# A second mixture with three sets of groups as rows by expert, the first of them placed and sent inside the attentions

## The chip, the cores and the metric

The kernel runs on one core of one Trainium2 chip. The metric is the time of one execution on the device in microseconds (us). Nine runs of the kernel before lie between 1503.12 and 1531.77 us, with a median of 1510.65.

## The reference

A decoder of two layers works on 32 batches of 128 tokens with 128 features, in float32. Each layer is three sub-layers with a residual each: a self-attention, a cross-attention with a context, and a mixture of experts. The change is in the mixture of the second layer, and in when its first part is prepared:

```python
x2 = hidden_states.reshape(-1, 128)                  # 4096 tokens, after the layer norm
logits = x2 @ gate_w.T                               # 16 experts
_, sel = top_k(logits + expert_bias, 4)
rw = softmax(logits taken at sel)                    # 4 shares for each token
out = swiglu(x2, shared) + sum over e of g[:, e] * swiglu(x2, expert e)   # g: rw put at sel
```

`swiglu(x, wg, wd, wu)` is `silu(x @ wg.T) * (x @ wu.T) @ wd.T`, with matrices of 128 x 128. Every token needs only 4 of the 16 experts; the reference computes them all and multiplies by the share, which is 0 for the other 12.

## The kernel before

**Units.** 4 batches (512 tokens) are a *group*, 8 groups in all; 2 groups (8 batches, `NBR`) are a *set*, sets 0 to 3. The residual `x[g]` of every group stays in SBUF.

**Dense or by rows.** The last layer has two ways to compute the mixture.
- *Dense*: for each group 16 *chunks*, one per expert. A chunk (`chunk_up`, `chunk_down`) is three products of a 128 x 128 matrix with the group's 512 columns (`pg`, `pu`, `y`), an ACT `Silu`, and two DVE products, the second with the `share` of the expert, which is loaded from DRAM already repeated over the partitions (`fetched`, 1 MB for four experts). A 17th chunk is the shared expert.
- *By rows*: the tokens of a set are copied to places ordered by expert. Routing on DVE (`route_rows`) gives four experts and shares per token; `placed` works out 4 places for each token with a chain of small PE and DVE operations and the expert that owns each tile of 128 rows (`owner`). `way_out` sends the tokens with 32 indirect DMAs (four for each batch, issued by POOL) to `rows_in` in DRAM. That table has 48 tiles of 128 rows, 12 *quads* of four tiles. For each quad `rows_of` loads four tiles (256 KB) and, after reading the owner of each tile into an SP register, that expert's three matrices (192 KB a tile), all on SP's queue; `rows_turned`, `rows_up` and `rows_down` transpose (`prows`), multiply by three matrices (`pg`, `pu`, `pyrows`, 128 columns per tile) and store to `rows_out` (on ACT's queue). `way_back` fetches each token's four results with 32 more indirect DMAs, and `added` multiplies by the shares and adds them to `x` on DVE. The group's shared chunk is still needed (`alone`).

Before the change sets 1 and 2 go by rows (`SETS = (1, 2)`), sets 0 and 3 are dense.

**Order.** `steps` writes the order of the instructions out by hand: a list of stages, each with its first step, its distance and its count; `between` stages are filled in piece by piece between the others. In `last_layer` steps 0 to 14 take two dense chunks each while sets 1, 2 and 3 are normed (`norm`, `scaled`), turned (`turn`), routed (`routing`, `chosen`), placed and sent; from step `Q0 = 15` on each step takes one quad and one dense chunk; then the rest of the dense chunks and the `alone` ones follow. Set 0 is routed (softmax) and its shares written to DRAM inside `second_layers`, the steps of the two attentions of the second layer, so that its dense chunks can start when the attentions end. In those attentions POOL copies the values to their spread form (`v`, line 1070), computes factors of norms (`r`), half of the normed tiles, and a check of the reciprocals (`in_range`, line 1309).

**Lines.** 974 is the helper `mm` of most matmuls, 1115 and below the helpers of the norms; 1290 to 1297 the averages of the attention; 2000 to 2033 the routing by rows, 2045 to 2077 the placing, 2080 the owners, 2088 the scatter, 2101 and 2109 the loads of rows and weights, 2117 to 2140 the quads, 2145 the gather, 2156 the adding, 2167 to 2170 the dense chunk.

Of the kernel before, what the change touches and what calls it, by code (L numbers as in the profile page):

```python
# [10 lines left out]
I32 = mybir.dt.int32  # L11
# [944 lines left out]
def fast_decoder(ctx: ExitStack, tc: tile.TileContext, ins, spans, out: bass.AP):  # L956
# [6 lines left out]
    st = ctx.enter_context(tc.tile_pool(name="st", bufs=4))  # L963
    kinds = {}
# [39 lines left out]
    F = load("fast", nc.sync)  # L1004
    ident = K["ident"]


    def load_wide(eng, *names):
        t = res.tile([128, sum(ins[n].shape[1] for n in names)], F32, name="wide")
        at, out = 0, []  # L1010
        for n in names:
            part = t[:, at : at + ins[n].shape[1]]
            at += ins[n].shape[1]
            out.append((_Pieces(part, spans[n]), lambda part=part, n=n: eng.dma_start(out=part, in_=ins[n])))
        return out

    (W0X, load_w0x), (W0F, load_w0f) = load_wide(nc.sync, "w0x", "w0f")
# [18 lines left out]
    ones_by_4 = res.tile([128, 4, 4 * HD], F32, name="ones_by_4")  # L1036
# [762 lines left out]
    def mixture(tag, W, route, per, last, weights_of):  # L1799
# [10 lines left out]
        def scaled(wk, g):  # L1810
            xn[g] = yield from normed(wk, g, *xn[g])
# [89 lines left out]
    def mixture_layer(tag, stages, more=()):  # L1901
# [36 lines left out]
    SETS = (1, 2)  # L1938
    NT = 4 * NBR + E
    QUADS = NT // 4  # L1940
    tables = ctx.enter_context(tc.tile_pool(name="tables", bufs=1, space=bass.MemoryType.DRAM))
    rows_in, rows_out = (
        {n: tables.tile([NT * S, D], F32, name=f"{name}{n}") for n in SETS} for name in ("rows_in", "rows_out")
# [10 lines left out]
    def last_layer(tag, W, stages, of_expert):  # L1954

        wk = phase(tag, mixture_psum)
        C = load("last", nc.scalar, wk)
        send, made = stages[5], stages[-1]
        hs, shares, NS = made["hs"], {}, made["NS"]
        one = wk.tile([128, 1], F32, name="one", bufs=1)  # L1960
        nc.vector.memset(one, 1.0)
        factors, xn, choices, ones, masks, parts, places, owners, held, ys, sgs, outs = ({} for _ in range(12))
# [5 lines left out]
        def scaled(g):  # L1968
            xn[g] = wk.tile([128, GB, D], F32, name="xr", bufs=2 * len(SETS) + 2)
            yield from normed(wk, g, *factors.pop(g), xn[g], nc.vector)  # L1970
# [14 lines left out]
        def routing(n):  # L1985
            lg = sm([128, NBR, E], "logits")
            for i, g in enumerate(of_set(n)):
                for b in range(GB):
                    mm(lg[:, i * GB + b, :], lhsT=hs[g][:, bass.ts(b, S)], rhs=W["r"], start=True, stop=True)
            choices[n] = route_rows(lg, n) if n in SETS else route_softmax(lg, edge)  # L1990
            next(choices[n])
# [6 lines left out]
        def route_rows(lg, n):  # L1998
            s = wk.tile([128, NBR, E], F32, name="s", bufs=1)
            nc.vector.tensor_copy(s, lg)  # L2000
            yield
            v = wk.tile([128, NBR, E], F32, name="v", bufs=1)
            nc.vector.tensor_tensor(v, s, rep(P["expert_bias"], NBR, 1), ALU.add)
            yield
            best = yield from greatest(v)

            ones[n] = wk.tile([128, 4, NBR, E], F32, name="ones", bufs=1)
            for k in range(4):
                nc.vector.tensor_tensor(ones[n][:, k], v, rep(best[:, :, k], E, 2), ALU.is_equal)
                yield  # L2010

            mask = masks[n] = wk.tile([128, NBR + 1, E], F32, name="mask", bufs=1)
            nc.vector.memset(mask[:, NBR], 0.0)
            nc.vector.tensor_tensor(mask[:, 0:NBR], v, rep(best[:, :, 3], E, 2), ALU.is_ge)
            yield
            raw = parts[n] = wk.tile([128, 4, NBR], F32, name="parts", bufs=len(SETS))
            t = wk.tile([128, 4, NBR, E], F32, name="picked", bufs=1)
            nc.vector.tensor_tensor(t, ones[n], rep(s, 4, 1), ALU.mult)
            yield
            nc.vector.tensor_reduce(raw, t, AX.X, ALU.add)  # L2020
            yield
            by_batch = raw.rearrange("p k b -> p b k")
            top = st.tile([128, NBR], F32, name="rtop")
            nc.vector.tensor_reduce(top, by_batch, AX.X, ALU.max)
            nc.vector.tensor_tensor(raw, raw, rep(top, 4, 1), ALU.subtract)
            yield
            nc.scalar.activation(raw, raw, AF.Exp)
            yield
            den = st.tile([128, NBR], F32, name="den")
            nc.vector.tensor_reduce(den, by_batch, AX.X, ALU.add)  # L2030
            nc.vector.reciprocal(den, den)
            yield
            nc.vector.tensor_tensor(raw, raw, rep(den, 4, 1), ALU.mult)

        def placed(n):

            mask = masks.pop(n)

            pp = sm([128, NBR + 1, E], "places")
            mm(pp, lhsT=C["below"], rhs=mask, start=True, stop=False)  # L2040
            for b in range(NBR):
                rhs = rep(mask[:, b], NBR - b, 1)
                mm(pp[:, b + 1 :], lhsT=one.to_broadcast([128, 128]), rhs=rhs, start=False, stop=(b == NBR - 1))
            pos = wk.tile([128, NBR + 1, E], F32, name="pos", bufs=1)
            nc.vector.tensor_copy(pos, pp)
            yield
            tiles = wk.tile([128, E], F32, name="expert_tiles", bufs=1)
            t = wk.tile([128, E, 8], F32, name="over", bufs=1)
            nc.vector.tensor_tensor(t, rep(pos[:, NBR], 8, 2), rep(C["tiles"], E, 1), ALU.is_gt)
            yield  # L2050
            nc.vector.tensor_reduce(tiles, t, AX.X, ALU.add)
            yield
            ends = wk.tile([128, E], F32, name="expert_ends", bufs=1)
            t = wk.tile([128, E, E], F32, name="upto", bufs=1)
            nc.vector.tensor_tensor(t, rep(K["desc16"], E, 1), rep(K["desc16"], E, 2), ALU.is_ge)
            yield
            nc.vector.tensor_tensor(t, t, rep(tiles, E, 1), ALU.mult)
            yield
            nc.vector.tensor_reduce(ends, t, AX.X, ALU.add)
            yield  # L2060
            nc.vector.tensor_tensor(tiles, ends, tiles, ALU.subtract)
            slot = pos[:, 0:NBR]
            nc.vector.scalar_tensor_tensor(slot, rep(tiles, NBR, 1), float(S), slot, ALU.mult, ALU.add)
            yield
            t = wk.tile([128, 4, NBR, E], F32, name="picked", bufs=1)
            nc.vector.tensor_tensor(t, ones.pop(n), rep(slot, 4, 1), ALU.mult)
            yield
            slots = wk.tile([128, 4, NBR], F32, name="slots", bufs=1)
            nc.vector.tensor_reduce(slots, t, AX.X, ALU.add)
            yield  # L2070
            places[n] = wk.tile([128, 4, NBR], I32, name="place", bufs=len(SETS))
            nc.vector.tensor_copy(places[n], slots)
            yield
            nc.vector.tensor_scalar(ends, ends, C["row"], None, ALU.is_le)  # L2074
            of = wk.tile([128, 1], F32, name="of", bufs=1)
            nc.vector.tensor_reduce(of, ends, AX.X, ALU.add)
            nc.vector.tensor_scalar(of, of, E - 1.0, None, ALU.min)
            yield
            pt = sm([1, S], "powner")
            nc.tensor.transpose(pt, of, ident)  # L2080
            owners[n] = wk.tile([1, S], I32, name="owner", bufs=len(SETS))
            nc.vector.tensor_copy(owners[n], pt)


        def way_out(n, u):
            b, g = u % GB, n * NBR // GB + u // GB
            for k in range(4):
                sent = nc.gpsimd.indirect_dma_start(  # L2088
                    out=rows_in[n],
                    out_offset=bass.IndirectOffsetOnAxis(ap=places[n][:, k, u : u + 1], axis=0),  # L2090
                    in_=xn[g][:, b],
                    in_offset=None,
                )

                tc.declare_no_dep(sent.ins, group=f"rows{n}", reason="rows of different places")
                tc.add_to_no_dep_group(f"rows{n}", sent.ins)
                nc.gpsimd.nop()
# [92 lines left out]
        at = {}  # L2190
        Q0 = 15
        todo = list(dense)
        for s in range(Q0):
            at[s] = [todo.pop(0) for _ in range(2)]
        s = Q0
        while s < Q0 + len(quads) + 1 and todo:
            at[s] = [todo.pop(0)]
            s += 1
        while todo:
            at[s] = [todo.pop(0) for _ in range(min(2, len(todo)))]  # L2200
            s += 1
        s = max(s, Q0 + len(quads) + 1)
# [409 lines left out]
```

## Time and profile before

| | |
|---|---|
| median of nine runs | 1510.65 us |
| the profiled execution | 1512.41 us, span 1510.6 us |
| PE busy | 1311.5 us (87%) |
| DVE, ACT, POOL busy | 874.0, 575.9, 470.5 us |
| moved by DMA | 114.41 MB, 76 GB/s over the span |
| indirect DMAs on POOL | 64 to `rows_in`, 64 from `rows_out` |
| mean granted TensorE clock | 0.938 |

The profile is of one execution. A row of a time line gives the start in us, the length, the engine, the source line, the operation, out<-in, and in brackets how long the engine was idle before and what ended that. "remote" stands where no recorded operation ends the wait. `PEld` is the weight load of PE, which lies beside its matmuls. A float32 matmul is recorded as two.

The first layer ends and the mixtures change at about 800 us; from 800 to 1104 us run the two attentions of the second layer, and from 1104 to the end the last layer.

### The profile page before, as it was taken

Reading aid. Unit: us, or ns where it says so; the run is one execution under the profiler, and the core shown is the slowest. Engines: PE = TensorE matmul, PEld = TensorE weight load, DVE = VectorE, ACT = ScalarE, POOL = GpSimd, SP = SyncE. Lnnn points to the kernel's source line nnn. Section 1 sums busy time; section 2 is a strip of 40 time slices with the busy share of each in tenths; the row PEclk is TensorE's granted clock in tenths of the full one; section 3 lists DMA queues with packets and bytes.
Section 4 is the critical chain, followed back from the end, with each engine's and each line's share of the span. In section 5 each row is a group of like instructions: output and inputs, shape, how many; then the busy total and the mean of one; then the engine's idle time right before and its main releaser. Section 6 shows DMA issues by size and latency. Waiting matters only on the chain. (4 is left out here: it accounts for less than half of the span.)

```text
span 1510.6 us, 27025 instructions
## 1 busy us (share of the span) xinstructions
PE 1311.5 (87%) x10598; PEld 842.8 (56%) x10598; DVE 874.0 (58%) x2256; ACT 575.9 (38%) x846; POOL 470.5 (31%) x665
## 2 busy tenths in 40 slices
PE   3699999999999986999998998898797474997896
PEld 2367777777777764444444665665443242765643
DVE  5656767768686653865754667675466252333453
ACT  2354545454454332333323455554531121332321
POOL 5324343333422311310001444542205425004343
PEclk7799999999999997999999999999898686999998
DMA  9201211111121124354152000000042302897812
GB/s 346 62 1 30 55 33 30 30 30 30 30 48 40 30 56 98 69 113 91 33 103 89 2 2 2 2 1 2 1 159 88 99 16 101 261 271 216 243 52 65
DMA packets 90422, 114.41 MB, mean 76 GB/s; under 512 B 7664, under 2 KB 73840, under 8 KB 87856
## 3 DMA queue, kind: packets, MB, share of 16 engines
q1 hardware_dynamic: 71936, 95.24, 23.1%
q0 software_dynamic: 4096, 8.40, 1.9%
q10 hardware_dynamic: 14256, 8.97, 1.9%
q8 instruction: 86, 1.41, 0.4%
q14 instruction: 48, 0.39, 0.1%
HBM read 93.05 MB, written 19.53 MB: 75 GB/s over the span
## 5 line engine op out<-in xcount | busy, mean ns | idle before, releaser
L974 PE MATMUL y<-sg,wide 128*128 128x512 f32 x288 | 156.3, 630 | 25.3 <-DVE sg L2170 18.2
L974 PE MATMUL pg<-hx,wide 128*128 128x512 f32 x288 | 154.1, 617 | 17.6 <-issue 16.2
L974 PE MATMUL pu<-hx,wide 128*128 128x512 f32 x288 | 152.1, 610 | 3.7 <-DVE sg L2168 3.7
L1275 ACT ACTIVATE e<-scores 128x1024 f32<-128x1024 f32 x128 | 124.0, 1021 | 56.9 <-PE scores L974 56.9
L2168 DVE TENSOR_TENSOR sg<-sg,pu 128x512 f32<-128x512 f32 x72 | 49.3, 685 | 141.5 <-PE pu L974 79.9
L2145 POOL DMA_INDIRECT back<-rows_out,place x64 | 62.6, 977 | 161.8 <-PE pg L974 88.9
L974 PEld LDWEIGHTS y<-sg,wide 128*128 128x128 f32 x288 | 49.8, 197 | 94.3 <-DVE sg L1880 36.3
L1121 POOL TENSOR_SCALAR xn<-x,mv,r 128x128 f32<-128x128 f32 x84 | 70.8, 850 | 91.6 <-PE pxn L1130 82.8
L1290 DVE STREAM_TRANSPOSE by_token<-sums 128x512 f32<-128x512 f32 x64 | 45.6, 713 | 91.7 <-PE sums L974 91.4
L974 PEld LDWEIGHTS pu<-hx,wide 128*128 128x128 f32 x288 | 55.9, 196 | 75.2 <-issue 67.5
L2167 ACT ACTIVATE sg<-pg 128x512 f32<-128x512 f32 x72 | 42.6, 597 | 139.7 <-PE pg L974 83.8
L1526 ACT ACTIVATE e<-xscores 128x1024 f32<-128x1024 f32 x64 | 62.0, 1021 | 79.9 <-PE xscores L974 79.9
L974 PEld LDWEIGHTS pg<-hx,wide 128*128 128x128 f32 x288 | 53.2, 199 | 66.5 <-issue 62.6
L974 PE MATMUL scores<-qb,k 32*128 32x512 f32 x512 | 78.2, 682 | 12.0 <-ACT qb L1461 4.5
L1877 ACT ACTIVATE sg<-pg 128x512 f32<-128x512 f32 x72 | 43.0, 597 | 119.0 <-PE pg L974 110.1
L974 PE MATMUL sums<-e,v 128*32 128x128 f32 x2048 | 74.5, 287 | 12.7 <-POOL v L1070 10.6
L1878 DVE TENSOR_TENSOR sg<-sg,pu 128x512 f32<-128x512 f32 x72 | 49.3, 685 | 60.8 <-PE pu L974 58.1
L2088 POOL DMA_INDIRECT rows_in<-xr,place x64 | 62.3, 973 | 65.0 <-DVE expert_ends L2074 46.1
L974 PEld LDWEIGHTS sums<-e,v 128*32 128x32 f32 x2048 | 55.4, 114 | 41.5 <-issue 16.5
L1092 POOL TENSOR_SCALAR r<-mv 128x4 f32<-128x4 f32 x48 | 11.5, 240 | 208.3 <-DVE mv L1111 207.9
L974 PE MATMUL po<-e,v 128*64 128x128 f32 x1024 | 66.2, 281 | 8.9 <-DVE v L1540 8.9
L1574 ACT COPY av<-po 128x512 f32<-128x512 f32 x64 | 37.5, 586 | 90.8 <-PE po L974 90.7
(280 smaller groups left out, 2769.2 us busy)
## 6 DMA issues: line engine op xcount, KB each, us to landing
row_weights<-in_w1f_dram SPq DMA_DIRECT2D x96, 192.0 KB
factor<-factors SPq DMA_DIRECT2D x64, 256.0 KB
share<-combined SPq DMA_DIRECT2D x32, 512.0 KB
share<-combined SPq DMA_DIRECT2D x16, 1024.0 KB
rows_in<-in_few SPq DMA_DIRECT2D x24, 256.0 KB
rows<-rows_in SPq DMA_DIRECT2D x24, 256.0 KB
rows_out<-yrows ACTq DMA_DIRECT2D x24, 256.0 KB
wide<-in_w1f_dram SPq DMA_DIRECT2D x1, 3272.0 KB
```

Source lines behind the costliest of these rows:

```text
L974: last[0] = nc.tensor.matmul(*args, **kw)
L1121: eng.tensor_scalar(n[:, b, :], x[g][:, b, :], mv[:, b, 0:1], r[:, b : b + 1], ALU.subtract, ALU.mult)
L1275: nc.scalar.activation(e[-1], ps[:, bass.ts(n, 2)].rearrange("p c i s -> p (c i) s"), AF.Exp, scale=scale)
L1290: nc.vector.transpose(tt.rearrange("p i t r -> p (i t r)"), po.rearrange("p i s -> p (i s)"))
L1526: nc.scalar.activation(e[-1], ps[:, n].rearrange("p r c s -> p (r c) s"), AF.Exp, scale=scale)
L1574: nc.scalar.copy(avs[w][n][:, :, bass.ts(b, S)], po)
L1877: nc.scalar.activation(sg, pg, AF.Silu)
L1878: nc.vector.tensor_tensor(sg, sg, pu, ALU.mult)
L2088: sent = nc.gpsimd.indirect_dma_start(out=rows_in[n], out_offset=bass.IndirectOffsetOnAxis(ap=places[n][:, k, u : u + 1], axis=0), in_=xn[ ...
L2145: nc.gpsimd.indirect_dma_start(out=outs[n, u][:, k], out_offset=None, in_=rows_out[n], in_offset=bass.IndirectOffsetOnAxis(ap=places[n][:, ...
L2167: nc.scalar.activation(sg, pg, AF.Silu)
L2168: nc.vector.tensor_tensor(sg, sg, pu, ALU.mult)
```

## The change

`SETS` becomes `(0, 2, 3)`; set 1 alone is dense. The tables, the routing and the placing move from `last_layer` into a class `Tables`, whose tiles lie in pools that live across both stages; the placing's large temporaries take buffers of the first attention (`rot`, `rotsin`), and set 0's normed tokens lie in the unused end of the `wide` weight tile. Set 0 is routed by rows, placed and sent inside `second_layers` (`placed` at step 37, `owned` and `way_out` from 39 on); its shares are no longer sent to DRAM. In `last_layer` the quads of set 0 start at step 1; sets 2, 1 and 3 are normed, turned, routed, and sets 2 and 3 placed and sent, beside them; the dense chunks of set 1 start at step 8, one per step to 23, one in three steps to 36, then two per step; six shared chunks end it. `filled`, which initializes `rows_in` in the first layers, has three tables instead of two (12 more DMAs of 256 KB). Some constants move to a pool that is closed after the first layers.

```diff
-    SETS = (1, 2)
+    SETS = (0, 2, 3)
...
+        def kept(self, g):
+            self.xn[g] = self.spare[:, g]
+            return self.xn[g]
...
+            ones, t = self.two_wide()
+            self.ones[n] = ones, t
...
         dense = [(g, c) for g in range(NG) if g * GB // NBR not in SETS for c in range(E + 1)]
         alone = [(g, E) for g in range(NG) if g * GB // NBR in SETS]
         quads = [(n, q) for n in SETS for q in range(QUADS)]
-        at = {}
-        Q0 = 15
-        todo = list(dense)
-        for s in range(Q0):
-            at[s] = [todo.pop(0) for _ in range(2)]
-        s = Q0
-        while s < Q0 + len(quads) + 1 and todo:
-            at[s] = [todo.pop(0)]
-            s += 1
-        while todo:
+        NQ = len(quads)
+
+        at, todo = {}, list(dense)
+        for s in range(8, NQ + 1):
+            if s < 2 * QUADS or s % 3 == 0:
+                at[s] = [todo.pop(0)]
+        for s in range(NQ + 2, 100):
+            if not todo:
+                break
             at[s] = [todo.pop(0) for _ in range(min(2, len(todo)))]
...
-            (each(rows_turned, quads), Q0, 1, len(quads)),
-            (several(turn, g1), 2, 1, 1),
-            once(routing, n1, 2),
-            (several(turn, g2), 8, 1, 1),
-            once(routing, n2, 8),
-            (several(turn, g3), 11, 1, 1),
-            once(routing, n3, 11),
-            (lambda _: send(wk, n3), 15, 1, 1),
+            (several(each(rows_of, quads), (0, 1)), 0, 1, 1),
+            (each(rows_turned, quads), 1, 1, NQ),
+            (several(turn, of_set(n2)), 2, 1, 1),
+            once(routing, n2, 2),
+            (several(turn, of_set(dense_n)), 3, 1, 1),
+            once(routing, dense_n, 4),
+            (lambda _: send(wk, dense_n), 6, 1, 1),
+            once(tables.owned, n2, 6),
+            (several(turn, of_set(n3)), 9, 1, 1),
+            once(routing, n3, 9),
+            once(tables.owned, n3, 14),
             (ups, 0, 1, LAST),
-            (each(rows_down, quads), Q0 + 1, 1, len(quads)),
-            (each(rows_up, quads), Q0, 1, len(quads)),
+            (each(rows_down, quads), 2, 1, NQ),
+            (each(rows_up, quads), 1, 1, NQ),
...
+                (each(rows_of, quads[2:]), 1, 1, NQ - 2),
...
+                once(tables.placed, n2, 4),
...
+                *((each(tables.way_out, batches(n2)[i : i + 4]), 5 + i // 4, 1, 4) for i in (0, 4)),
...
+                once(tables.placed, n3, 12),
+                (each(tables.way_out, batches(n3)), 15, 1, NBR),
+                (each(way_back, batches(0)), 23, 1, NBR),
+                (each(added, batches(0)), 25, 1, NBR),
+                (each(way_back, batches(n2)), 31, 1, NBR),
+                (each(added, batches(n2)), 33, 1, NBR),
+                (each(way_back, batches(n3)), NQ + 3, 1, NBR),
+                (each(added, batches(n3)), NQ + 5, 1, NBR),
```

In `second_layers`:

```diff
-            (first(send), 43, 1, 1, choose),
+            (lambda _: tables.owned(0), 39, 1, 1, placed),
...
-                (lambda _: choose(0, 3), 26, 1, 13),
+                (lambda _: choose(0, 3), 29, 1, 7),
+                (placed, 37, 1, 1),
+                (lambda u: tables.way_out(0, u), 39, 1, NBR),
```

`Tables.route`, `placed`, `owned` and `way_out` are the former `route_rows`, `placed` and `way_out` operation by operation, with the owners' transposition as a stage of its own.

## The prediction

> **What bounds the kernel now.** I read the page first for the whole, then the windows table cut at the places where the work changes, then the time lines of the engines inside those stretches. The columns of the windows are: stretch, its length, busy time of PE, PEld, DVE, ACT and POOL, granted clock, DMA share, GB/s.
>
> ```profile
> PE 1311.5 (87%) x10598; PEld 842.8 (56%) x10598; DVE 874.0 (58%) x2256; ACT 575.9 (38%) x846; POOL 470.5 (31%) x665
> 800.00:1104.00 304.00, 265.18 (x3166) 168.96 (x3164) 181.10 (x496) 154.96 (x209) 108.83 (x174) 0.94 0.04 13
> 1104.00:1282.00 178.00, 117.06 (x335) 59.04 (x336) 78.85 (x229) 32.85 (x51) 69.25 (x77) 0.80 0.27 95
> 1282.00:1441.00 159.00, 140.65 (x801) 102.82 (x800) 57.53 (x103) 55.05 (x94) 30.58 (x32) 0.96 0.82 242
> 1441.00:1510.00 69.00, 55.62 (x156) 26.84 (x154) 31.79 (x63) 14.26 (x24) 31.97 (x32) 0.92 0.19 55
> ```
>
> PE is the busiest engine, but the change lies in the last layer, the last three rows, where PE idles 61, 18 and 13 us. The first of them is the opening: dense chunks run while sets 1 and 2 are routed and sent. The second is the 24 quads, with DMA at 0.82. The third is the tail, as long as the last 32 gathers on POOL.
>
> One step of the quad stretch (PE; start, length, operation):
>
> ```profile
> 1308.06 0.60 PE L2117 MATMUL prows<-in_few,rows 128*128 128x128 f32 x4
> 1308.50 1.02 PE L974 MATMUL pg<-hx,wide 128*128 128x512 f32 x2
> 1309.36 1.02 PE L974 MATMUL pu<-hx,wide 128*128 128x512 f32 x2
> 1310.22 1.05 PE L974 MATMUL pyrows<-row_weights,sgrows 128*128 128x128 f32 x8
> 1311.11 1.16 PE L974 MATMUL pg<-hrows,row_weights 128*128 128x128 f32 x8
> 1312.11 1.06 PE L974 MATMUL pu<-hrows,row_weights 128*128 128x128 f32 x8
> 1313.00 1.02 PE L974 MATMUL y<-sg,wide 128*128 128x512 f32 x2
> 1313.87 0.60 PE L2117 MATMUL prows<-in_few,rows 128*128 128x128 f32 x4
> ```
>
> By start to start a dense chunk is 0.86 + 0.86 + 0.87 = 2.59 us, a quad 0.44 + 0.89 + 0.89 + 0.89 = 3.11 us. PE has no gap here: a step with both is 5.7 to 5.8 us, and 12 steps from 1289.34 to 1364.93 took 75.6, so 6.30 each with their waits for loads.
>
> Next, SP's time line (issue time only), POOL's, and what stands still while POOL issues indirect DMAs (brackets: idle before, releaser):
>
> ```profile
> 1200.60 0.38 SPq L2101 DMA_DIRECT2D rows<-rows_in  x1
> 1201.77 4.34 SPq L2109 DMA_DIRECT2D row_weights<-in_w1f_dram  x4
> 1185.37 0.96 POOL L2088 DMA_INDIRECT rows_in<-xr,place  x1 [0.30 <-issue]
> 1185.96 0.29 DVE L2000 COPY s<-logits 128x128 f32<-128x128 f32 x1 [18.44 <-remote]
> 1190.85 0.60 ACT L2167 ACTIVATE sg<-pg 128x512 f32<-128x512 f32 x1 [21.87 <-remote]
> 1191.50 2.07 PE L974 MATMUL pg<-hx,wide 128*128 128x512 f32 x2 [16.16 <-issue]
> 1378.06 0.60 ACT L2129 ACTIVATE sgrows<-pg 128x512 f32<-128x512 f32 x1 [9.29 <-remote]
> 1379.61 0.69 DVE L2130 TENSOR_TENSOR sgrows<-sgrows,pu 128x512 f32<-128x512 f32 x1 [11.29 <-remote]
> 1380.36 2.07 PE L974 MATMUL pyrows<-row_weights,sgrows 128*128 128x128 f32 x8 [7.85 <-DVE sgrows L2130]
> 1103.51 0.51 POOL L1309 TENSOR_SCALAR in_range<-rec 128x64 f32<-128x64 f32 x1 [10.38 <-DVE rec L1292]
> ```
>
> An indirect DMA costs POOL 0.96 + 0.30 = 1.26 us, 32 of them 40 us. Late in every such burst ACT and DVE stand still although their inputs are done: DVE's copy waits 18.4 us for logits finished at 1170.1. I call that a freeze. It costs PE 16.2 + 3.7 = 20 us in the first scatter (1152 to 1193), 7.5 + 12.8 = 20 in the second (1233 to 1274). During the gathers of set 1 nine steps (1364.93 to 1435.34) took 70.4 us, 7.82 each: 13.7 us over the nine at 6.30.
>
> **The change part by part.**
>
> *PE work.* Dense chunks, the shared ones counted, fall from 68 + 4 to 34 + 6: 32 x 2.59 = 83 us off. Twelve quads more: 37 us. One more `places` group (1138.10 to 1140.04): 2 us. Net -44 us; the rest of the gain or loss is in the waits.
>
> *Attentions' end.* Set 0 is routed as rows and placed there. By the rows of set 1 the placing chain is 4.7 us of DVE (1146.17 to 1152.28 less two dense products), the longer routing some 3 us, and in the instruction order 16 statistics pairs at 0.40 (6.3 us) now stand there too. DVE was busy 10 of 29 us from 1075 to 1104, so most fits; but POOL now has 20 indirect DMAs (25 us) ahead of its last `in_range`, between the `v` copies that the last averages wait for. The last `v` stands behind 17 of them (21 us): POOL's rows from 1078 on, strung in the new order, put it at 1106, where it was made at 1092.84 and used at 1100.43. With 2 us for DVE I take the last average 8 us later, at 1111; bounds 0 (all hidden) and 25 (a freeze as above).
>
> *The new wait.* In the order the last 12 of set 0's 32 scatters stand behind that `in_range`, so they run after the attentions: 1.3 + 12 x 1.26 = 16.4 us. The first `rows` load waits on SP for the last; behind it queue all weight loads. PE's next instruction is the transposition of these rows, with set 2's turn and routing behind it. From the end of the second scatter (1273.6) to its rows on PE (1282.0) were 8.4 us. First quad on PE: 1111 + 16.4 + 8.4 = 1136; 1140 with a short freeze; bounds 1126 and 1156. The opening of 178 us becomes 36 us of which PE idles about 25.
>
> *36 quad steps.* From the step lists 21 carry a dense chunk, 15 none. With chunk: 21 x 6.30 = 132 (bounds 5.8 and 6.6). Without: PE needs 3.1 us, but SP issues a quad's loads in 1.17 + 3 x 1.14 + 0.45 = 5.04 us, or 5.6 as it ran from 1200.60; DMA moves 1.31 MB per quad, at the 284 GB/s of the busiest stretch 4.6. So SP sets these steps: 15 x 5.5 = 83 (bounds 5.0 and 5.8). Idle of 2.4 us per step also touches the clock: a wait of 7.85 us was followed by 2.07 us for a group of 1.05, one of 1.95 by groups of 1.75 and 1.91; at that price a quad takes 5.9, hence my upper bound.
> [...]
>
> *Bursts inside the steps.* Scatters of sets 2 and 3 (steps 5 to 9 and 15 to 22) and gathers of 0 and 2. A scatter cost 20 us under dense work; here two quads are loaded ahead and PE can catch up in steps that SP sets, so I take 15, 30 for both (bounds 0 and 60). Gathers: 13.7 and, under steps mostly without chunk, 10: 24 (bounds 14 and 28).
> [...]
>
> *Tail.* 13 dense and 6 shared chunks, 49 us, beside 32 gathers at 1.25 with waits for their buffers: as before, 69 us (bounds 65 and 75).
>
> *Free.* Twelve more fills of `rows_in` in the first layers lie under DMA at 0.23 share; uncovered they cost 12 x 0.8 = 10 us. Tile and pool moves cost nothing: the same instructions on other addresses. ACT's table loads stay as many.
>
> *Sum.* 1140 + 132 + 83 + 30 + 24 + 69 = 1478 of span, against 1510.6. The profiled execution took 1512.41, 1.8 over its span, and lies 1.8 above the median of 1510.65; so 1478 as a median.
>
> **The rivals.** *Freezes hidden* (quads loaded ahead cover them, attentions delayed little): 1128 + 132 + 83 + 14 + 69 = 1426. For it: PE needs only 3.1 of 5.5 us in 15 steps, and the first scatter of a set is split in short bursts. Against: SP too stood still from 1373 to 1378. *No change*: a full freeze at the attentions' end and 20 per scatter: 1156 + 132 + 83 + 40 + 24 + 69 = 1504. *Slower*: a scatter inside the quad steps stops the whole chain, because ACT, DVE and SP all serve it, for its whole 40 us: 1140 + 132 + 83 + 80 + 24 + 69 = 1528. For it: in the dense openings other chunks lay ready, in the quads nothing does. It decides above 35 us per scatter (1448 without scatters, 1518 being the edge). *The change not doing what it says* is partly so already: 12 of 32 scatters of the first set stand outside the attentions; that is in the sum.
>
> **How the numbers follow.** Forecast 0.56, hidden 0.21, no change 0.10, slower 0.13. Under 0.5%, 7.5 us, this kernel's times tell nothing apart; both the forecast and the hidden case are faster by more: 0.77; within it 0.10; slower 0.13. The range reaches 11 us below the hidden case (15 steps without chunk at their bound of 5.0 and the tail at 65) and above the no-change case to 1515; left out are the rest of the hidden case and the slower one, 0.18.
>
> **What would show it.** Right: the last layer's first `prows` near 1140 with PE idle before it; steps without chunk near 5.5 us with PE waiting on `rows` or `row_weights`; PE busy about 1268; indirect DMAs 192 instead of 128; the last quad near 1409. Wrong: PE idle over 30 us in one scatter; first `prows` after 1156; steps with chunk above 7; or quad steps that run at 4 us, which would mean that SP's issue is no bound.

## The result, and the profile after

The changed kernel takes 1560.09 us (median of 20 runs, 1548.86 to 1576.71), the kernel before 1511.02 beside it (62 runs): a ratio of 1.033, interval 1.031 to 1.035. It is slower; the forecast was 1478. The profiled execution took 1554.93 us with a span of 1553.1.

One fact is needed to read every later number. The experiments ran on several chips, and these are of two sorts. On five of them (9, 11, 13, 14 and 6) the kernel before takes 1441.8 to 1442.8 us; on three (1, 5 and 12) it takes 1508 to 1522, as in the runs of the result. Chips 11 and 5 were used twice, and each was of the same sort both times. I call the second sort the *freezing* chips, for a reason that the traces show. Each ratio below is against the kernel before on the same chip.

The page of the changed kernel, its busy times and the shares of its chain:

```profile
PE 1282.0 (83%) x10753; PEld 859.8 (55%) x10753; DVE 853.1 (55%) x2256; ACT 576.8 (37%) x848; POOL 531.9 (34%) x729
PE 15%; another core or an unknown queue 7%; DVE 2%; issue 1%; ACT 1%; DMA 1%; POOL 1%; SPq 0%; ACTq 0%; DVEq 0%
```

PE has 29.5 us less to do than before and the span is 42.5 us longer, so PE idles 72 us more. The unknown releaser in the chain, 7% of the span, is a first hint: time in which the end waits for something that no instruction explains.

The windows of the last layer of the changed kernel, cut at its first quad, at both scatters of sets 2 and 3 and at the last quad (columns as in the prediction; the stretch between the scatters is left out):

```profile
1144.19:1187.21 43.02, 33.12 (x202) 30.45 (x202) 19.84 (x83) 15.76 (x23) 2.55 (x5) 0.78 0.71 195
1187.21:1233.78 46.57, 14.13 (x69) 11.23 (x69) 3.36 (x12) 6.20 (x11) 30.81 (x32) 0.65 0.36 111
...
1274.67:1339.70 65.03, 17.14 (x89) 13.15 (x88) 5.93 (x11) 5.81 (x10) 42.28 (x44) 0.61 0.33 96
1339.70:1391.56 51.86, 51.86 (x307) 38.01 (x307) 17.92 (x27) 21.30 (x36) 0.00 (x0) 0.99 0.90 259
1391.56:1482.00 90.44, 63.06 (x380) 52.32 (x379) 32.65 (x77) 24.00 (x42) 46.33 (x49) 0.86 0.75 214
1482.00:1553.00 71.00, 59.19 (x170) 28.45 (x168) 35.24 (x75) 15.39 (x27) 34.51 (x36) 0.96 0.22 64
```

The second and the third row hold the loss. In the second POOL issues the 32 indirect DMAs of set 2, in the third the 32 of set 3 and, with no pause, the first 12 gathers of set 0. Two quads take 46.6 us there and three take 65.0, with PE busy 14 and 17 us. In the fourth row POOL issues nothing, PE has no idle time at all, and nine steps with a chunk take 51.9.

The time lines of the changed kernel in these two rows, and its first quad:

```profile
1144.19 1.08 PE L2160 MATMUL prows<-in_few,rows 128*128 128x128 f32 x4 [19.24 <-DMA rows<-rows_in]
1196.15 0.60 PE L2160 MATMUL prows<-in_few,rows 128*128 128x128 f32 x4
...
1213.15 0.59 ACT L2162 COPY hrows<-prows 128x512 f32<-128x512 f32 x1 [14.84 <-remote]
1226.51 0.96 POOL L2086 DMA_INDIRECT rows_in<-xr,place  x1 [0.30 <-issue]
1232.06 0.59 ACT L2182 COPY yrows<-pyrows 128x512 f32<-128x512 f32 x1 [18.32 <-remote]
...
1281.86 11.26 SPq L2152 DMA_DIRECT2D row_weights<-in_w1f_dram  x4
1321.94 0.69 DVE L2173 TENSOR_TENSOR sgrows<-sgrows,pu 128x512 f32<-128x512 f32 x1 [39.53 <-remote]
1322.69 2.07 PE L977 MATMUL pyrows<-row_weights,sgrows 128*128 128x128 f32 x8 [36.74 <-issue]
```

PE finishes the transposed rows at 1196.75, and ACT copies them at 1213.15. The trace also records when PE's semaphore was raised; these are its updates in the scatter of set 2 (us):

```
1194.99 1195.58 | 1205.43 1213.13 1222.94 1228.53 | 1232.04 1232.08 1232.12 1232.16 1232.21 1232.30 1232.36 1232.40 1232.44
```

So ACT did not stand still by itself: the news that PE was done reached it 16 us late. From about the seventh indirect DMA on, PE's updates come one in 5.6 to 9.9 us (in the scatter of set 3 up to 21.7 us lie between two); POOL's last indirect DMA of the row ends at 1227.5, and 4.6 us later nine updates come 0.04 to 0.09 us apart. ACT's copy starts 20 ns after the update at 1213.13, its next operation 20 ns after the one at 1232.04.

Between the recorded end of `prows` and its update lie 16.4 us; what fills them, the trace does not show.

PE is not alone in this. Between its loads SP runs register operations, which wait for no product of PE. Six of its instructions in a row start at 1207.50, 1208.90, 1209.60, 1210.30, 1211.70 and 1212.40, in steps of 0.70 us or twice that. From 1340 to 1390 us, where POOL issues nothing, its register operations take 0.02 to 0.16 us in the same execution, its loads into registers 0.26 us and more. The five long gaps between PE's updates above (9.85, 7.70, 9.81, 5.59 and 3.51 us) are 14, 11, 14, 8 and 5 times 0.70. What makes these steps, and whether PE and SP share it, the traces do not tell. DVE's and ACT's news to PE is not late here: PE starts 0.05 us after DVE's `sgrows` ends at 1206.21, and 0.05 us after ACT's `hrows` ends at 1213.74.

### The profile page after: what moved, and what is told of

It reads as the page before. It is cut to its first block, busy times and chain, and to the rows that moved or that the text cites. A ratio compares the mean times of both kernels' runs of the same rounds, so it can differ in the third digit from the quotient of the medians.

```text
span 1553.1 us, 27804 instructions
## 1 busy us (share of the span) xinstructions
PE 1282.0 (83%) x10753; PEld 859.8 (55%) x10753; DVE 853.1 (55%) x2256; ACT 576.8 (37%) x848; POOL 531.9 (34%) x729
## 3 DMA queue, kind: packets, MB, share of 16 engines
q0 software_dynamic: 6144, 12.60, 2.8%
## 5 line engine op out<-in xcount | busy, mean ns | idle before, releaser
L2188 POOL DMA_INDIRECT back<-rows_out,place x96 | 92.2, 961 | 124.4 <-DVE x L2199 96.1
L977 PE MATMUL y<-sg,wide 128*128 128x512 f32 x224 | 120.2, 625 | 9.2 <-DVE sg L2213 3.4
L2173 DVE TENSOR_TENSOR sgrows<-sgrows,pu 128x512 f32<-128x512 f32 x36 | 24.7, 687 | 187.4 <-ACT sgrows L2172 89.7
L977 PE MATMUL pu<-hx,wide 128*128 128x512 f32 x224 | 115.1, 595 | 1.1 <-issue 1.1
L977 PE MATMUL pg<-hx,wide 128*128 128x512 f32 x224 | 115.8, 599 | 0.0
L977 PE MATMUL pyrows<-row_weights,sgrows 128*128 128x128 f32 x288 | 47.6, 318 | 80.1 <-issue 41.7
L977 PEld LDWEIGHTS pyrows<-row_weights,sgrows 128*128 128x128 f32 x288 | 43.5, 225 | 94.5 <-issue 52.1
L1882 ACT ACTIVATE sg<-pg 128x512 f32<-128x512 f32 x72 | 43.0, 597 | 119.3 <-PE pg L977 112.0
L1883 DVE TENSOR_TENSOR sg<-sg,pu 128x512 f32<-128x512 f32 x72 | 49.3, 685 | 61.0 <-PE pu L977 58.2
L977 PEld LDWEIGHTS pu<-hx,wide 128*128 128x128 f32 x224 | 42.5, 191 | 54.0 <-issue 51.8
L1545 DVE COPY v<-pval 128x512 f32<-128x512 f32 x64 | 43.5, 680 | 50.9 <-PE pval L977 50.9
```

The costliest lines, as they stand in the source:

```text
L977: last[0] = nc.tensor.matmul(*args, **kw)
L1545: nc.vector.tensor_copy(v[:, bass.ts(n, XC), :], pv)
L1882: nc.scalar.activation(sg, pg, AF.Silu)
L1883: nc.vector.tensor_tensor(sg, sg, pu, ALU.mult)
L2173: nc.vector.tensor_tensor(sg, sg, pu, ALU.mult)
L2188: nc.gpsimd.indirect_dma_start(out=outs[n, u][:, k], out_offset=None, in_=rows_out[n], in_offset=bass.IndirectOffsetOnAxis(ap=places[n][:, ...
```

## The experiments

### The chips: the same kernel twice

The first four variants ran where nothing freezes, so that they price other things; the changed kernel itself was then run beside the kernel before.

Absolute times of two profiles can be apart before their kernels differ: one and the same operation (the 141st that writes `e` on ACT) starts between 872.6 and 885.2 us in the profiles of the changed kernel and its variants, which do the same work up to there. Where it matters for a comparison below, it is said.

> The changed kernel again, beside the kernel before on the chip of this call. In the call before this one the kernel before took 1442.8 us, 68 us less than its 1510.7 elsewhere, and no variant of the changed kernel showed a freeze. Theory (the freezes belong to the chip that runs, not to the program alone): where the kernel before takes about 1443 this one takes 1445 to 1455 with no wait of PE over 10 us inside the quad steps; where it takes about 1511, 1560 with waits of over 30 us. Rival (leaving out or altering the scatters of sets 2 and 3 is what took the time off): 1500 or more beside 1443.

> The kernel before, for its trace on the chip of this call. Theory (freezes belong to the chip): where it takes about 1442, the two scatters of sets 1 and 2 show no wait of PE over 5 us, the last layer's first stretch is some 40 us shorter than its 178 and the quads' stretch some 14 us shorter than its 159. Rival (the chip is faster throughout): every stretch is shorter by some 4.5 per cent, the first 1104 us too.

The changed kernel took 1451.6 us beside 1441.8: ratio 1.0048 (1.0010 to 1.0085). Of this run, the windows of the first quads, of set 2's scatter and of the tail:

```profile
1139.07:1182.01 42.94, 32.70 (x202) 29.98 (x202) 19.85 (x83) 15.56 (x23) 2.54 (x4) 0.78 0.71 196
1182.01:1225.00 42.99, 32.46 (x187) 25.08 (x188) 12.49 (x37) 14.70 (x25) 31.38 (x32) 0.81 0.80 268
...
1383.00:1445.90 62.90, 55.19 (x169) 27.35 (x167) 35.31 (x75) 15.55 (x27) 35.98 (x36) 0.98 0.24 74
```

The same 32 indirect DMAs, 1.26 us apart, now leave PE 32.5 of 43 us busy, and PE waits for nothing longer than 8.0 us in them (for the dense set's routing). And of the kernel before, span 1440.0 on such a chip, the window of the opening that the prediction showed:

```profile
1104.00:1282.00 178.00, 153.51 (x587) 88.31 (x588) 93.30 (x250) 50.49 (x82) 70.13 (x77) 0.91 0.48 163
```

PE is busy 153.5 us of the 178 where it was busy 117; its second quad starts at 1234.0 instead of 1282.0, so the same window holds more work. Up to 1104 us both chips run alike (PE busy 999.5 and 998.2 us), so the chip is not faster throughout. The opening is 48 us shorter (40 expected), the quads 14 (as expected) and the tail 9. One wait inside a scatter is over the expected 5 us, 8.7 us for the placing, and it stands on both sorts of chip. From there on the kernel before takes 336 us instead of 407, the changed one 342 instead of 449. By this the freezes cost the kernel before 71 us and the changed one 107, in the spans of the profiles (69 and 108 by the medians).

### Without the scatters of sets 2 and 3

```diff
-            for k in range(4):
+            for k in range(4 if n == SETS[0] else 0):
```

> The changed kernel (1560.1 us) without the 64 indirect DMAs of sets 2 and 3; their rows keep the filling of before, so the quads multiply other numbers in the same time. Theory (scatters inside the quad steps stop the chain): the 2 steps of 46.6 us become 2 of 6, the 3 of 65.0 us become 3 of 6 with some 10 us for the 12 gathers of set 0 that now stand alone: 71 us off, 1489. Rival (the steps themselves are longer than summed: turns, routing and placing of three sets in them): the scatters only lie beside it, under 25 us off, 1535 or more.

> The changed kernel without the 64 indirect DMAs of sets 2 and 3 (their rows keep the filling), beside the changed kernel itself. Where the kernel before takes about 1443: within 10 us of the changed kernel, since nothing freezes. Where it takes about 1511: theory 70 us under the changed kernel, 1490; rival (step contents) under 25 us.

Neither ran where anything freezes. 1446.2 (ratio 1.0002, 0.9964 to 1.0040) and 1446.1 (1.0008, 0.9970 to 1.0046), 5 us under the changed kernel: without freezes these 64 indirect DMAs lie beside the quads almost free. The first expectation, 71 us off, took the freezes for granted and does not apply to this chip.

### Fewer bytes, another form, pauses

`half_rows` sends 64 numbers of each row, `plain` replaces the indirect DMA by a plain one from the same queue, `gap4` pauses. For sets 2 and 3, inside and behind the loop of `way_out`:

```diff
 half_rows:
+                    out=rows_half[n],
+                    in_=self.xn[g][:, b, 0 : D // 2],
 plain:
+                    at = (4 * u + k) * S
+                    sent = nc.gpsimd.dma_start(out=rows_in[n][at : at + S, :], in_=self.xn[g][:, b])
 gap4:
+            if n != SETS[0]:
+                for _ in range(4):
+                    nc.gpsimd.tensor_scalar(self.pad, self.pad, 1.0, None, ALU.mult)
```

> The changed kernel with the indirect DMAs of sets 2 and 3 as many as before, each row cut to its first 64 numbers and sent to a tensor of its own (the quads read their filling). Theory (number of indirect DMAs in a row): freezes as before, 1545 to 1560. Rival (bytes): the freezes halve, some 35 us off, 1525.

> The changed kernel with each indirect DMA of sets 2 and 3 replaced by a plain DMA of the same 64 KB from the same queue, POOL's, to consecutive rows (the quads then multiply rows in another order). Theory (it is the indirect form's issue by POOL): no freeze, 1490. Rival (any DMA that POOL issues, or the bytes): PE waits as before, 1540 to 1560.

> The changed kernel with four POOL products of 128x128 on a tile of their own (0.85 us each by xn's row, 3.4 us) after every 4 indirect DMAs of sets 2 and 3: as many DMAs and bytes, POOL busier than before, but never more than 4 in a row. Theory (a row of more than some 8 indirect DMAs holds PE's semaphore updates back, a pause lets them through): no wait of PE over 8 us inside the scatters, 71 us off; set 2's scatter now takes 68 us and its first rows are wanted some 35 us after its start, so 25 of these come back as a wait for rows: 1515. Rival (the 512-byte rows' traffic, or POOL being busy): the same bytes, POOL busier: 1545 to 1570.

On the chip of these three nothing freezes: 1447.4 (1.0043, 1.0006 to 1.0081), 1450.4 (1.0036, 1.0000 to 1.0073) and 1460.8 (1.0109, 1.0040 to 1.0179). They show only that pauses cost 9 us there beside the changed kernel's 1451.6; the expectations that count on freezes do not apply. Each then ran on a freezing chip.

> The changed kernel with the rows of sets 2 and 3 cut to 64 numbers on their way out (as many indirect DMAs, half the bytes), for the case that this call's chip has the freezes. There, theory (the number of indirect DMAs in a row): PE's waits inside the two scatters as long as in the changed kernel, 30 us and more, 1545 to 1565. Rival (the bytes): half of it, near 1525. Where the kernel before takes 1442: 1447 as before.

1553.6 beside 1509.1, one run each. The freezes are as long as ever. The window of the second scatter, and PE in it:

```profile
1275.00:1340.00 65.00, 17.42 (x93) 13.20 (x92) 6.68 (x14) 5.80 (x10) 42.23 (x44) 0.63 0.28 80
```
```profile
1324.47 2.07 PE L977 MATMUL pyrows<-row_weights,sgrows 128*128 128x128 f32 x8 [36.69 <-issue]
```

Half the bytes change nothing: 36.69 us where the whole rows had 36.74. The bytes are not the cause; the number of rows, 128 in each DMA, was kept.

> The changed kernel with the indirect DMAs of sets 2 and 3 replaced by plain DMAs of the same 64 KB, from the same queue, POOL's, for the case that this call's chip has the freezes. There, theory (the issue of indirect DMAs, one after the other): no wait of PE over 10 us inside the two scatters, the gathers alone freezing, 1475 to 1500. Rival (whatever POOL issues in a long row): 1545 to 1565. Where the kernel before takes 1442: 1450 as before.

1499.4 (one run) beside a kernel before of 1508.1, 61 us under the changed kernel's 1560.1. POOL's time line and PE's waits during these DMAs:

```profile
1193.43 16.10 POOL L2095 DMA_DIRECT2D rows_in<-xr  x30
```
```profile
PE pct L1849 <- DVE comb L1800: 8.0, 1, 8.0
PE pyrows L977 <- DVE sgrows L2177: 1.4, 1, 1.4
```

Thirty plain DMAs in a row from POOL, 0.54 us each, and PE's longest wait is the one for the routing that it has without freezes too. POOL's queue moves packets of the same size in both kernels, 2.05 KB: 1370 with 2.81 MB here from 1187 to 1230 us, 6144 with 12.60 MB in all in the changed kernel. So by these runs it is neither POOL's queue, nor its packets or bytes, but the indirect form. (A plain DMA needs no places, so set 3's go out right behind set 2's, by 1240 us; this moves the time, not what freezes.) In the same execution the first 12 gathers, which are indirect, bring PE a wait of 8.5 us. The time is at the upper end of the expected 1475 to 1500; the gathers, still indirect, go on to hold the later quads up.

> The changed kernel with four POOL products (3.4 us) after every 4 indirect DMAs of sets 2 and 3, once more, for the case that this call's chip has the freezes (kernel before near 1511, not 1442). There, theory (a long row of indirect DMAs holds PE's semaphore updates back, a pause lets them through): 1515 or less, no wait of PE over 15 us inside those scatters. Rival (POOL's indirect DMAs hold them back however they are spaced): 1555 or more. Where the kernel before takes 1442: 1461 as before, the pauses costing 10.

1506.2 beside 1521.7, one run each. PE's waits from the start of set 2's scatter to the end of set 3's, first with the pauses:

```profile
PE pct L1849 <- DVE comb L1800: 8.0, 1, 8.0
PE pg L977 <- issue: 1.9, 1, 1.9
PE pyrows L977 <- DVE sgrows L2178: 1.7, 2, 1.5
```

and in the changed kernel:

```profile
PE pyrows L977 <- issue: 36.7, 1, 36.7
PE pyrows L977 <- DVE sgrows L2173: 24.1, 2, 14.6
PE pg L977 <- ACT hrows L2162: 12.5, 2, 11.1
PE pg L977 <- issue: 5.5, 1, 5.5
```

The last four sum to 79 us, but they run on to 1340, over the 12 gathers behind set 3's scatter. Up to 1345, which is as far behind the same gathers, the kernel with the pauses has these waits of the same kinds:

```profile
PE pg L977 <- issue: 5.6, 2, 3.7
PE pyrows L977 <- issue: 1.8, 2, 1.3
PE pyrows L977 <- DVE sgrows L2178: 1.7, 2, 1.5
PE pg L977 <- ACT hrows L2167: 0.4, 1, 0.4
```

That is 9.5 us with a pause of 2.4 to 2.9 us (the four products were shorter than expected) after every 4 indirect DMAs, 5.4 of them beside the gathers, which have no pauses; 8.6 go to rows that come later. POOL issues as many indirect DMAs and does more besides. So their number alone does not count, but how they follow each other. Whether that is the length of the row or the density is not separated: the pauses also stretch set 2's 32 from 40 to 58 us. And a break can be too short. At the attentions' end of the changed kernel POOL copies a `v`, 0.30 us, after 5 indirect DMAs at most, and DVE still stands still for 14.0 us (until 1115.71); between PE's updates at 1102.86 and 1115.68 lies none.

### The steps' own work

Where nothing freezes the changed kernel still misses the forecast's gain. `early_turn` moves work out of the first quad steps:

```diff
-            (several(turn, of_set(n2)), 2, 1, 1),
-            once(routing, n2, 2),
-            (several(turn, of_set(dense_n)), 3, 1, 1),
+            (several(turn, of_set(n2)), 1, 1, 1),      # ahead of rows_turned
+            once(routing, n2, 1),
+            (several(turn, of_set(dense_n)), 1, 1, 1),
```

> The changed kernel with the turning of sets 2 and of the dense set and set 2's routing put ahead of the first quad in PE's order (their statistics and rows one step earlier, set 2's choice and placing one step earlier). In the changed kernel PE waits 19.7 us for the first rows and then gives 8 to 10 us between quads to these turns at the lower clock. Theory (part of the missing gain is work that the sum left out: turns and routing inside the first quad steps): 8 us under the changed kernel; beside a kernel before of 1442 that is 1440 to 1445, beside one of 1511, where a scatter freezes, 1550. Rival (the first steps wait for loads or for the routing on DVE, not for PE): no difference, 1447 to 1452, or 1560.

1438.2 beside 1441.9: ratio 0.9977 (0.9943 to 1.0011), where the changed kernel had 1.0048. PE's time line:

```profile
1113.29 2.29 PE L1135 MATMUL pxn<-in_few,xr 128*128 128x128 f32 x8 [1.20 <-DVE xr L1126]
...
1131.93 1.09 PE L2160 MATMUL prows<-in_few,rows 128*128 128x128 f32 x4 [10.36 <-DMA rows<-rows_in]
```

The turns fill 8 us of the wait for the first rows, and the last quad ends at 1367.7 instead of 1382.2. The theory holds, by the medians with 13 us instead of 8. By the profiles it is the 8: of the 14.7 us between the spans 7.5 lie ahead of all that differs (872.6 against 880.1 at the operation named above), and from the first quad to the last it takes 236.0 us instead of 243.4.

`early_place` also places and sends set 0 three steps earlier:

```diff
-                (placed, 37, 1, 1),
-                (lambda u: tables.way_out(0, u), 39, 1, NBR),
+                (placed, 34, 1, 1),
+                (lambda u: tables.way_out(0, u), 36, 1, NBR),
```

> early_turn with set 0 placed three steps earlier in the attentions (its choice in 5 pieces a step instead of 3) and sent from step 36 instead of 39, so that all 32 indirect DMAs stand ahead of the last in_range on POOL. In early_turn PE waits 10.4 us for the first rows, behind 12 indirect DMAs that stand after it. Theory (the late rows of set 0 are what is left of the opening): first quad on PE near 1120 instead of 1132, 10 us under early_turn: beside a kernel before of 1442 that is 1428. Rival (DMA, at 0.92 share from 1225 on, takes it back): the first quad is earlier and the last is not, 1436 to 1440.

1431.4 beside 1442.6: 0.9917 (0.9879 to 0.9955), ahead of the kernel before. But not by the reason given. The first quad came at 1137.9, not near 1120, and the last at 1368.5; the profiled span is 1432.7, that of `early_turn` 1431.2. This execution was 8.8 us behind that of `early_turn` before the two kernels differ (881.4 against 872.6). With that taken off the first quad is 2.8 us earlier instead of 12, and the span 7.3 us shorter, 5 of them between the first quad and the last (230.9 us for 236.0), for which no run shows the cause. POOL became the bound of the attentions' end:

```profile
1093.08 1.27 PE L1135 MATMUL pxn<-in_few,xn 128*128 128x128 f32 x3 [5.17 <-POOL xn L1126]
```

The indirect DMAs stand ahead of POOL's own `xn` and `v`. Whether this kernel is really ahead of `early_turn` stays open: their intervals overlap and they ran on different chips.

### Both together

`early_gap` is `early_turn` with the pauses of `gap4`.

> early_turn (turns of set 2 and the dense set ahead of the first quad, set 2 placed one step earlier) together with gap4 (four POOL products after every 4 indirect DMAs of sets 2 and 3). Where the kernel before takes about 1442: early_turn's scatter starts 30 us earlier, so that the pauses no longer make the first rows of set 2 late; 1438 to 1443. Where it takes 1511 to 1522, theory (pauses let PE's semaphore updates through): 13 us under gap4's 1506, 1485 to 1495, the first kernel here under the kernel before by more than 1 per cent there. Rival (the freeze comes back since the scatter now lies beside set 2's first loads): 1515 or more.

> early_turn with the pauses after every 4 indirect DMAs of sets 2 and 3, for the case that this call's chip has the freezes. There, theory: 1485 to 1495, 1 to 2 per cent under the kernel before; rival (the freezes return as soon as the scatter lies beside other loads): 1515 or more. Where the kernel before takes 1442: 1446 as before.

Where nothing freezes 1446.2, 8 us over `early_turn` and more than expected: ratio 1.0022 (0.9996 to 1.0048). On a freezing chip 1494.7 beside 1508.1: 0.9881 (0.9826 to 0.9937), within the expected 1485 to 1495 and ahead of the kernel before.

`early_gap_both` pauses between the gathers of sets 0 and 2 as well, in `way_back`:

```diff
+            if n != SETS[-1]:
+                for _ in range(3):
+                    nc.gpsimd.tensor_scalar(tables.pad, tables.pad, 1.0, None, ALU.mult)
```

> early_gap with three POOL products after every 4 gathers of sets 0 and 2 as well. Where the chip has the freezes, theory (a row of gathers holds PE's semaphore updates back as a row of scatters does, and a pause lets them through): the waits of 5 to 8 us for sgrows in the quads' second half go, 15 to 20 us under early_gap's 1494.7. Rival (the gathers' waits come from their rows, not from their issue): no change, or longer, since POOL has 29 us more to do and the tail ends with its gathers. Where the kernel before takes 1442: 1446 to 1456, the pauses being cost alone.

> early_gap_both once more, for the case that this call's chip has the freezes: 1475 to 1480 beside a kernel before of 1508 (theory: pauses between gathers let PE's updates through), 1495 or more (rival: gathers wait for their rows). Where the kernel before takes 1442: 1464 as before, the pauses costing 18.

Where nothing freezes 1464.2 (1.0164, 1.0093 to 1.0235), worse than expected. On a freezing chip 1493.2 (two runs; 0.9864, 0.9703 to 1.0024): no better than `early_gap`. The theory holds for the quads and the rival for the end: the quads' second half loses its waits (for `sgrows` 3.9 us after 1300 us instead of 16.4, first to last quad 250 us instead of 272), and the tail, which ends with POOL's gathers, grows from 71 to 89 us.

## Why the prediction was wrong

The sum was 1140 + 215 + 54 + 69. The runs give each term, on the freezing chip and, for the changed kernel itself, without freezes:

| term | predicted | freezing | without |
|---|---|---|---|
| first quad on PE | 1140 | 1144.2 | 1139.1 |
| 36 quad steps | 215 | 244 (taken from the right) | 244 |
| scatters and gathers in them | 54 | 94 (the rest of 338) | 0 |
| tail | 69 | 71 | 63 |
| span | 1478 | 1553 | 1446 |

*First quad.* Right in size, by errors that cancel in part: the last averages came 12 us later than summed (POOL's `in_range` waits until 1123.5; the freeze at the attentions' end was in the bounds, and 4 us were allowed for a short one), and the rows were on PE 4.2 us after the last scatter's end instead of 8.4. The 12 us are the freeze: without it `in_range` starts at 1118.6 in an execution that was 7 us behind near 875 us, so the 1111 of the sum was right there.

*Scatters inside the steps: the step that failed.* I took 15 us each, less than the 20 of the dense opening, "here two quads are loaded ahead and PE can catch up". Set 2's took 46.6 us for two quads that need 14.5 without freezes, so 32; set 3's, with 12 gathers right behind, 65.0 for three that need 17, so 48. What is loaded ahead is of no use: in each quad the news of a PE product must reach ACT or DVE three times (`prows`, `pg` and `pu`, `pyrows`), and the next product waits for their answer. My slower rival said this, with 40 us for each scatter, and its point of decision, 35 us, was passed: the mean of 32 and 48 is 40. That it is just 40 is partly chance, since the 48 belong to one row of 44, scatter and gathers, and the gathers have a term of their own. The rival had 0.13, though the rows shown spoke for it: ACT and DVE stood still in three bursts out of three, and only dense products whose inputs lay ready had kept PE busy in between.

*The steps.* 215 was wrong by 29, for two reasons of opposite sign. Both prices were too high: steps with a chunk took 5.76 us where nothing disturbed them, not 6.30, and without freezes the eight steps without one behind step 23 took 3.2 to 6.8, on the mean 4.7, not 5.5. SP's issue, 5.04 us a quad in the prediction, does not bound single steps; three quads of buffers let the loads run ahead in the longer ones. But the first twelve steps also hold the turns of three sets, three routings, the placing and the dense set's shares; none of that was in the sum. Without freezes the first five steps took 37 us (27.5 summed) and the next seven 66 (42.5 summed). `early_turn` shows that a part of it can be had back. The order of the instructions had named all of these operations; I priced the steps from a stretch that held none.

*Gathers and tail.* 24 predicted; the last twelve quads took 90.4 us against 66 without freezes, so 24. With the 80 of the scatters that is 104, not the 94 of the table: some 11 us were made good between the bursts, in steps that were shorter than in the run without freezes (four quads in 31.8 us for 38.5, nine in 52.1 for 56.9). Tail 71 for 69. *Free* was right: up to 1104 us PE's busy time is that of before within a few us (993.0 and 998.2), and the same `e` on ACT starts at 873.2 where it started at 874.7.

*The clock.* In the first quad steps PE waited 2.21 us (for `mask`, until 1167.4). The granted clock stayed at 1.00 until 1170.0, while PE ran narrow products (`places`, `logits`), and was 0.50 until 1176.9, where groups that take 1.05 us took 2.06 and 1.91. From 1160 to 1170 PE's other waits are 0.26 us at most. So here the clock fell with no wait over 2.21 us in the 10 us ahead of it, and in the row of the prediction groups of 1.75 and 1.91 us stand behind a wait of 1.95 us; what part the narrow products had is not shown.

*SP.* The prediction read that SP "stood still" in a burst, from 1373 to 1378. It did not stand: its register operations went on there in steps of 0.70 us. In the scatter of set 2 two times four weight loads took 8.18 and 15.27 us to issue, against 4.50 and 4.37 without freezes; in that of set 3 four took 11.26.

With the scatters at 80 in place of 30 the sum would have been 1528, with the steps' 29 as well 1557; the span was 1553. Without any freeze the two kernels differ by half a per cent: there the 32 chunks saved, the 12 quads more, and the steps' extra work about cancel.

## What to carry to other kernels

A stop that hits the messages between engines costs what the waiting chain has no other work for (here 32 and 48 us in the two scatters beside quads, 20 beside dense chunks): before moving a burst beside a new kind of work, count how many passages between engines one unit of that work has, not how much of it is loaded ahead. Price a step from everything that the order puts into it, not from a stretch in which the rare items are missing. Where indirect DMAs stand in long rows beside such work, break the rows up or use a plain form (here 1506.2 and 1499.4 us on freezing chips, the changed kernel 1560.1), and measure on more than one chip: early turns and pauses together gave 1.2 per cent over the kernel before on one sort of chip, and on the other the pauses cost 8 us.

## What the runs showed of the hardware

In the profile of the changed kernel PE's semaphore updates come late from about the seventh indirect DMA of a row from POOL on in one scatter and the tenth in the other, one in 5.6 to 9.9 us in the former and up to 21.7 us apart in the latter, until 4.6 to 5.1 us after the row's end. SP's instructions start in steps of 0.70 us then, and PE's gaps in the first of the two are whole multiples of that. By the time of the kernel before, three chips of eight are of this sort (1508 to 1522 us) and five are not (1441.8 to 1442.8). In the profile of the changed kernel on one of the five (13), with the same instructions at the same distances of 1.26 us, PE waits at most 8.0 us behind the first quad; in the first profile it waits up to 36.7 us. A pause of 2.4 to 2.9 us after every 4 is enough against most of it (9.5 us of PE's waits are left of 79), a copy of 0.30 us after every 5 or fewer is not (DVE stands still for 14.0 us). Half the bytes per row change nothing (a wait of 36.69 us for 36.74), and beside 30 plain DMAs of 64 KB from POOL, in packets of the same 2.05 KB, 0.54 us each where an indirect one takes 1.26, PE's longest wait is 8.0 us. What inside the chip holds the updates back, and why only on some chips, stays open. Every time here is that of a recorded execution, so it is open too whether the recording has a part in it.
